# A four-layer graph network on one core: ones multiplied first, x rows a group ahead, feeds put off, ranks before a layer's end, the 20-row block first

## The chip, the cores and the metric

The kernel runs on one core of one Trainium2 chip. The metric is the time of one execution on the device in microseconds; the median over several runs is given. The core's engines, each with its own queue of instructions, are TensorE (PE in the profile; its weight loads are PEld), VectorE (DVE), ScalarE (ACT), GpSimd (POOL) and SyncE (SP, which here only issues DMAs).

## The reference, cut to what matters

```python
# x: 2708 x 512 float32; adj: 2708 x 2708 of zeros and ones, symmetric, some 16 ones in a row
deg = max(sum(adj != 0, axis=-1), 1)
# layer 0
dinv = rsqrt(deg); a_norm = dinv * (adj + I) * dinv
x = layernorm(x + relu((a_norm @ x + x) @ W0 + b0))
# layer 1
dis = (adj.sum(1) + 1e-8) ** -0.5
x = layernorm(x + ((dis * adj * dis.T) @ x) @ W1.T + b1)
# layer 2: attention, twice
y = x
for W in W2_stack:                       # 512 x 1024 each
    Wh, Ws = split(y @ W, 2, axis=-1)
    y = leaky_relu((softmax(Wh @ Ws.T) * adj) @ Wh + y, 0.01)
x = layernorm(x + y)
# layer 3: eight heads that together are one 512 x 512 matrix
x = layernorm(x + adj @ (x @ W3) + b3)
```

## The kernel before

The 2708 nodes are 22 blocks of 128 rows; the last block, number 21, has only 20 rows in use. The columns of a result (nodes again) are worked on in six chunks (`CH`: four of 512, one of 384, one of 276), and for each chunk the source blocks come in six groups (`GROUPS`: four groups of four blocks, two of three). A step is one (layer, chunk k, group g). `step` (line 1043) writes out the work of every engine for that step by hand, and all instructions go through `OrderedEngine` (line 62; its calls are made in line 70, which is why the profile gives L70 for nearly everything). It ties each instruction to the one written before it on the same engine. So the order within each engine is the order of the program text; no scheduler changes it.

Layers 0, 1 and 3 have the same form. `load` (line 741) starts the DMAs of adjacency tiles `at`, two steps ahead of their use, on SP's queue; in layer 0 these are 256 KB tiles of float32, later pages of bytes from `masks`, which layer 0 writes itself. `prepare` (line 782) runs one step ahead: for each block ACT makes `m`, the adjacency tile in the form in which PE multiplies it; in the first chunk `halve` (line 713) also splits the block's rows x into a high part `xh` (on ACT) and a low part `xl` (on DVE). In layer 0 `examine` (line 814) makes bytes of the tiles (`some` on ACT, `bytes` on POOL), tests them (`odd` on DVE), and adds them up into `part`. In layer 1 `prepare` ends with `feeds`, a DVE reduction that notes which blocks feed which quarters of a block. `multiply` (line 849) then makes the products `acc<-m,xh` and `acc<-m,xl` on PE: four accumulators of a chunk, each a PSUM bank. There are two sets of four banks, used by even and odd chunks in turn.

`load_rows` (line 707) issues the DMAs of the x rows, in layers 0 and 1 on POOL's queue, where weights (`load_weights`, line 697), the residual rows `xres` and the rows `xt` of the transposed x are issued too.

When a chunk's last group is multiplied, `degrees` (line 886, layer 0) makes the degrees: products `deg` and `cnt` on PE, `dg` and `cnt_sb` from them on DVE, then xt times dg on POOL and an inverse square root on DVE. `evict` (line 919) adds accumulators and xt into `ht`. In the next chunk's steps `ends` (line 1079) goes through phases: phase 0 calls `project` (line 936: ht times the weights, `mm`; a block of 20 rows gives four partial sums in one bank), and phases 0 and 1 call `combine` (line 976: scale, bias and residual in `r` and `xres`) and `finish` (line 995: layernorm into `o`, and its DMA). Phase 2 of layer 1 turns the rows for the attention.

Beside layer 1's chunks, and beyond its end, `index` (line 1097) makes the lists by which the attention gathers its neighbours. It is a generator that yields in turn for DVE and for PE: DVE makes `up`, PE the product `rank`; DVE `keep`, `place` and another `up`, PE the product `rest`; DVE `place_r`, a test whose results go to `bad` by way of `top`, and then for each block `at_row`, `hit` and `both` (`one_hot`, line 1221), from which PE makes the product `list`. `work` (line 572) lets the first unfinished job go on by a step. `beat` (line 585) is called once a block in the attention's projections and calls `work` in two of three calls.

The attention's projections (`project_steps`, called in line 1684) make `wst`, which ACT copies, and `z`, whose copy `z_sb` is DVE's. The mixed weights (`mix`) that they need are the first products of the whole program, from weights `wt` that a DMA brings.

After the last layer's last chunk `run` (lines 568 to 570) projects its three blocks 19, 20 and 21, and combines, normalises and stores them one after the other.

Of the kernel before, what the change touches and what calls it, by code (L numbers as in the profile page):

```python
# [8 lines left out]
FP = mybir.dt.float32  # L9
FR = mybir.dt.float32r  # L10
BF = mybir.dt.bfloat16
# [3 lines left out]
ALU = mybir.AluOpType  # L15
# [498 lines left out]
class Fast:  # L514
# [17 lines left out]
    def run(self):  # L532
        kernel, nc = self.k, self.nc
        with ExitStack() as ctx:
            pool = lambda name, bufs, **kw: ctx.enter_context(
                self.tc.tile_pool(name=name, bufs=bufs, reuse_waits="tile", **kw)
            )
            self.pages, self.wides = pool("pages", PAGES), pool("wides", WIDES)
            self.small, self.lists = pool("small_f", 4), pool("lists", 1)
            self.banks = [pool(f"banks{h}", 4, space=PSUM) for h in range(2)]  # L540
            given = [kernel.x_in[bass.ts(i, P), :] for i in range(NB)]
            l0 = Layer(0, given, kernel.w0, kernel.b0)
            l1 = Layer(1, kernel.saved[0], kernel.w1, kernel.b1)
            l3 = Layer(3, kernel.saved[2], kernel.w3, kernel.b3)
            self.attention = attention = Attention(self)
            self.jobs, self.due, self.other, self.beats = [], None, 1, 0
            run = Run(l0, l1)
            for t in range(len(run.seq)):
                self.step(run, t)
            attention.project(attention.layers[0], 0)  # L550
            for g in range(3):
                self.ends(run, g)
                if g == 1:
                    attention.project(attention.layers[0], 1)


            run = Run(l3)
            run.seq = [(l3, k, g) for k in range(TWO) for g in range(4)]
            run.seq += [(l3, k, g) for g in (4, 5) for k in range(2)]
            run.seq += [(l3, k, g) for k in range(2, TWO) for g in (4, 5)]  # L560
            run.seq += [(l3, k, g) for k in range(TWO, len(CH)) for g in range(len(GROUPS))]
            attention.run(self.early(run))
            for j in range(*GROUPS[5]):
                l3.rows[j] = attention.made[j]
            for t in range(4 * TWO, len(run.seq)):
                self.step(run, t)

            ly, k = run.before
            for i, n, ps in self.project(ly, k):
                self.finish(ly, k, [(i, n, self.combine(ly, i, n, ps))])  # L570

    def work(self, engine):

# [131 lines left out]
        nc.gpsimd.dma_start(ly.bt, ly.bias.partition_broadcast(P))  # L705

    def load_rows(self, ly, j):
        if ly.rows[j] is None:
            ly.rows[j] = self.page(f"x{ly.number}_{j}")
            queue = self.nc.sync if ly.number == 3 else self.nc.gpsimd  # L710
            queue.dma_start(ly.rows[j], ly.source[j])
# [29 lines left out]
    def load(self, ly, k, g):  # L741
# [26 lines left out]
            ly.done["bytes", k, g] = at  # L768
        ly.done["at", k, g] = tiles
        if k == 0 and ly.number == 0:  # L770
            for j in range(*GROUPS[g]):
                self.load_rows(ly, j)
        if k == 0 and ly.number == 3 and g < 4:
            for j in range(*GROUPS[g]):
# [4 lines left out]
                self.nc.gpsimd.dma_start(xt[c][:, :cw], self.k.x_t[:, c, c0 : c0 + cw])  # L779
            ly.done["xt", k] = xt  # L780

    def prepare(self, ly, k, g):


        nc, (c0, cw) = self.nc, CH[k]
        ats = ly.done.pop(("at", k, g), None)
        if ats is None:
            return
        ms = []
        for j, at in zip(range(*GROUPS[g]), ats):  # L790
            if k == 0:
                self.halve(ly, j)
            m = self.page(f"m{ly.number}_{k}_{j}", FR)
            nc.scalar.copy(m[:, :cw], at[:, :cw])
            ms.append(m)
        ly.done["m", k, g] = ms
        if ly.number == 0:
            self.examine(ly, k, g, ats)
        if ly.number == 1:
            at, (j0, j1) = ly.done.pop(("bytes", k, g)), GROUPS[g]  # L800
            feeds = self.k.feeds.rearrange("p i q j -> p j (i q)")
            i0, full = c0 // QW, cw // QW
            sets = [(j0, j1, P)] if j1 < NB else [(j0, j1 - 1, P), (j1 - 1, j1, QW)]
            for q0, q1, n in ((0, full, QW), (full, -(-cw // QW), cw % QW)):
                for a, b, rows in sets if q0 < q1 else ():
                    v = at[:rows, a - j0 : b - j0, q0 * QW : q0 * QW + (q1 - q0) * n]
                    nc.vector.tensor_reduce(
                        feeds[:rows, a:b, i0 + q0 : i0 + q1],
                        v.rearrange("p j (q i) -> p j q i", i=n),
                        AX.X,  # L810
                        ALU.max,
                    )

    def examine(self, ly, k, g, ats):
        nc, cw = self.nc, CH[k][1]
# [67 lines left out]
                    stop=(j in stops and not first),  # L883
                )

    def degrees(self, ly, k, g):

        nc, cw = self.nc, CH[k][1]
        i0, n = CH[k][0] // P, len(blocks_of(k))
        if g == len(GROUPS) - 2:  # L890
            ly.both = both = self.page(f"both{k}", BF)
            if cw % P:
                nc.vector.memset(both, 0.0)
            nc.vector.tensor_add(both[:, :cw], ly.part[k][:, 0, :cw], ly.part[k][:, 1, :cw])
            return
        both = ly.both
        ps = self.bank(k + 1, f"deg{k}")
        nc.tensor.matmul(ps[:, :cw], self.k.ones_b, both[:, :cw], start=True, stop=True)
        pc = self.bank(k + 1, f"cnt{k}")
        for q in range(n):  # L900
            nc.tensor.matmul(
                pc[:, q : q + 1],
                both[:, bass.ts(q, P)],
                self.k.ones_b[:, 0:1],
                start=True,
                stop=True,
            )
        dg = self.page(f"dg{k}")
        nc.vector.tensor_scalar(dg[:, :cw], ps[:, :cw], 1.0, 1.0, ALU.max, ALU.add)
        cnt = self.small.tile([P, DC], FP, tag="cnt", name=f"cnt_sb{k}")[:, :n]  # L910
        nc.vector.tensor_copy(cnt, pc[:, :n])
        xt = ly.done["xt", k]
        for c in range(DC):
            nc.gpsimd.tensor_mul(xt[c][:, :cw], xt[c][:, :cw], dg[:, :cw])
# [21 lines left out]
    def project(self, ly, k):  # L936

        nc = self.nc
        parts = []
        for i, lo, n in blocks_of(k):  # L940
            if n <= QW:
                ps = self.few(
                    k,
# [32 lines left out]
    def combine(self, ly, i, n, ps):  # L976

        nc, x = self.nc, ly.done.pop(("xres", i))
        if n <= QW:
            t = self.page(f"mm_sb{ly.number}_{i}")  # L980
            self.total(t[:n], ps, n, D)
            ps = t
# [12 lines left out]
    def finish(self, ly, k, parts):  # L995
# [8 lines left out]
        for i, o, n in out:  # L1004
            if ly.number == 3:
                nc.sync.dma_start(self.k.out[i * P : i * P + n, :], o[:n])
            else:
                rows = n if ly.number else P
                nc.gpsimd.dma_start(self.k.saved[ly.number][i][:rows], o[:rows])
        return out  # L1010

    def before_products(self, run, t):

# [2 lines left out]
        if t == 0:  # L1016
            mixing = self.attention.mix(0)
            next(mixing)
            self.load(*seq[0])
            self.load(*seq[1])  # L1020
            self.k.constants(self.page)
            self.prepare(*seq[0])
        if t + 2 < len(seq):
            self.load(*seq[t + 2])
# [7 lines left out]
        if ly.number == 1 and k == 0 and g == 0:  # L1032
            for j in range(*GROUPS[4]):
                self.load_rows(ly, j)
        if t + 1 < len(seq):
            self.prepare(*seq[t + 1])
        if ly.number == 0 and g == len(GROUPS) - 2:
            self.degrees(ly, k, g)
        if t == 0:
            for _ in mixing:  # L1040
                pass
# [1 line left out]
    def step(self, run, t):  # L1043
# [21 lines left out]
        if g == len(GROUPS) - 1:  # L1065
            if ly.number == 3:
                self.biased(ly, k)
            if ly.number == 0:
                self.degrees(ly, k, g)
            while run.before and run.phase < 2:  # L1070
                self.ends(run, run.phase)
                run.phase += 1
            self.evict(ly, k)
            run.before, run.phase = (ly, k), 0
            if ly.number == 1:
                self.jobs.append((k, self.index(k)))
                self.work("DVE")

    def ends(self, run, g):

        nc, (ly, k) = self.nc, run.before
        if g == 0:
            run.parts = self.project(ly, k)
            run.x = []
        if g in (0, 1):
            some = run.parts[:2] if g == 0 else run.parts[2:]
            run.x += [(i, n, self.combine(ly, i, n, ps)) for i, n, ps in some]
# [9 lines left out]
    def index(self, k):  # L1097
# [79 lines left out]
        )  # L1177
        nc.vector.tensor_add(place, place, place_r)

        top = tile_("top", [P, n], FP)  # L1180
        nc.vector.tensor_mul(place_r, rank, rest[:, :, PAD:])
        nc.vector.tensor_reduce(top, place_r, AX.X, ALU.max)
        for q, (i, _, _) in enumerate(blocks_of(k)):
            room = sum(t >= nq * ONLY for ts in lists_of(i) for t in ts) * P
            nc.vector.tensor_scalar(
                kernel.bad[:, kernel.nbad + i : kernel.nbad + i + 1],
                top[:, q : q + 1],
                1.0 - room,
                0.0,
                ALU.add,  # L1190
                ALU.max,
            )
        whole, part = (self.page(f"{t}{k}", I32, one) for t in ("whole", "part"))
        row, which = tile_("row", one, BF), tile_("which", one, BF)
        nc.vector.tensor_scalar_add(whole, place, float(FAR))
# [4 lines left out]
        sums = tile_("sums", [P, n, 2 * LISTS], FP)  # L1200
        for q in range(n):
            rows, both = self.one_hot(i0 + q, row[:, q, :], which[:, q, :])
            yield "PE"
            ps = self.bank(self.other, f"list{i0 + q}", (P, 2 * LISTS))
            for j in range(NB):
# [69 lines left out]
class Attention:  # L1275
# [98 lines left out]
    def project_steps(self, ly, k):  # L1374
# [19 lines left out]
        for i, lo, n in blocks_of(k):  # L1394
# [8 lines left out]
            for c in range(DC if n > QW else 0):  # L1403
# [4 lines left out]
                    start=(c == 0),  # L1408
                    stop=(c == DC - 1),
                )  # L1410
            if n > QW:
                nc.vector.tensor_copy(z[:n], ps[:n])
            for b in range(2):
                nc.sync.dma_start(
# [429 lines left out]
```

## Time and profile before

| | us |
|---|---|
| timed, median of 3 runs | 2369.26 (2368.26 to 2371.22) |
| profiled execution, its own time | 2338.2 |
| its span | 2336.5 |
| PE busy in it | 2274.8 |
| DVE busy | 1474.8 |
| POOL busy | 762.3 |
| ACT busy | 662.2 |

The span reaches from the first to the last event that the profiler recorded; the profiled execution's own time has 1.7 us more. The profiled execution is another one than the timed ones. Busy times of the engines overlap. In a row of the timeline stand the start, the time, the engine, the line, the operation, output and inputs by their names, shapes and types, a count, and in square brackets the time that the engine was idle before it and what released it. PEclk is the clock that TensorE was granted, as a share of the full one.

In the span, layer 0 lies up to about 319 us, layer 1's products up to about 615, the end of layer 1 with the first attention layer's projections up to about 786. The attention's scores and sums follow, and layer 3 is last.

### The profile page before, as it was taken

What the parts mean: (1) busy time and instruction counts of PE and PEld (TensorE: products, weight loads), DVE (VectorE), ACT (ScalarE), POOL (GpSimd) and SP (SyncE); (2) the same over time, 40 slices, a digit from 0 to 9 for tenths busy, and PEclk for the clock granted to TensorE, in tenths of its full rate; (3) what the DMA queues carried; (4) which work ended last, traced back from release to release, by engine and by line L of the source; (5) the groups of instructions that cost most, each with busy time, mean ns of one, the idle gap of its engine ahead of it and who ended that gap; (6) DMA issues with size and microseconds to landing.
All of it is one profiled execution on the core that took longest, in us unless ns stands there. A gap on an engine that the chain in (4) does not pass through costs nothing.

```text
span 2336.5 us, 26171 instructions
## 1 busy us (share of the span) xinstructions
PE 2274.8 (97%) x8518; PEld 1292.5 (55%) x8518; DVE 1474.8 (63%) x2831; ACT 662.2 (28%) x1334; POOL 762.3 (33%) x879
## 2 busy tenths in 40 slices
PE   8999999999999999999999999999999999999997
PEld 6677677778644444443456444444443456566585
DVE  6999986786655529657677511228677788724523
ACT  6544353223100113222223200113232334432211
POOL 6645641111000000636375550000636466551000
PEclk9999999999999999999999999999999999999998
DMA  9765652222434404869699996405869799983311
GB/s 343 258 199 169 182 172 86 74 86 70 171 146 167 154 0 143 278 229 311 204 324 350 302 388 232 152 0 163 279 217 314 233 316 329 305 279 96 123 48 43
DMA packets 312440, 463.50 MB, mean 198 GB/s; under 512 B 60162, under 2 KB 189706, under 8 KB 312292
## 3 DMA queue, kind: packets, MB, share of 16 engines
q1 hardware_dynamic: 252276, 240.81, 31.5%
q0 software_dynamic: 60016, 220.92, 27.1%
q8 instruction: 69, 1.13, 0.2%
q14 instruction: 79, 0.65, 0.1%
HBM read 307.75 MB, written 153.85 MB: 198 GB/s over the span
## 4 chain that ended last, share of the span: by engine, by line
PE 84%; DVE 7%; DMA 4%; issue 2%; ACT 1%; POOL 1%; SPq 0%; DVEq 0%; ACTq 0%; POOLq 0%
PE sp L70 32%; PE acc L70 29%; PE mm L70 9%; PE z L70 6%; PE wst L70 6%; DMA pairs<-s 1%; DMA at<-in_adj_t 1%; DVE st L70 1%; DMA at<-mask 1%; ACT m L70 1%; DVE s L70 1%; PE list L70 1%; PE mix L70 0%; POOL bytes L70 0%; PE tr_x2t L70 0%
## 5 line engine op out<-in xcount | busy, mean ns | idle before, releaser
L70 POOL DMA_INDIRECT g<-pairs,givers x510 | 516.2, 1012 | 897.0 <-DMA pairs<-s 537.4
L70 PE MATMUL sp<-xs,wst_sb 128*128 128x512 f32 (+3 forms) x2112 | 797.7, 544 | 0.0
L70 PEld LDWEIGHTS sp<-xs,wst_sb 128*128 128x128 f32 (+1 forms) x2112 | 380.0, 186 | 406.8 <-issue 321.9
L70 PE MATMUL acc<-m,xh 128*128 128x512 f32 (+4 forms) x1584 | 571.4, 382 | 13.6 <-ACT m L70 7.0
L70 PE MATMUL acc<-m,xl 128*128 128x512 f32 (+4 forms) x1584 | 553.2, 367 | 1.5 <-DVE xl L70 1.5
L70 PEld LDWEIGHTS acc<-m,xh 128*128 128x128 f32 (+1 forms) x1584 | 290.3, 189 | 81.4 <-issue 22.3
L70 PEld LDWEIGHTS acc<-m,xl 128*128 128x128 f32 (+1 forms) x1584 | 290.3, 189 | 48.1 <-issue 5.7
L70 ACT COPY s<-sp 128x512 f32<-128x512 f32 (+2 forms) x252 | 133.6, 531 | 482.1 <-PE sp L70 469.5
L70 PE MATMUL acc<-g 128*32 128x512 f32 (+1 forms) x1020 | 260.8, 605 | 0.9 <-DMA g<-pairs,givers 0.5
L70 DVE TENSOR_TENSOR top<-top,s 128x512 f32<-128x512 f32 (+5 forms) x240 | 149.6, 623 | 170.6 <-ACT s L70 169.1
L70 PE MATMUL mm<-w,ht 128*128 128x512 f32 (+1 forms) x528 | 222.6, 593 | 8.1 <-DVE ht L70 8.1
L70 ACT CAST m<-at 128x512 fp32r<-128x512 uint8 (+5 forms) x396 | 199.2, 567 | 80.0 <-DMA at<-mask 63.7
L70 ACT ACTIVATE s<-s 128x512 f32<-128x512 f32 (+3 forms) x264 | 150.7, 580 | 236.6 <-DVE s L70 236.3
L70 DVE TENSOR_TENSOR sum<-sum,s 128x512 f32<-128x512 f32 (+4 forms) x252 | 157.4, 625 | 23.9 <-ACT s L70 23.9
L70 DVE TENSOR_TENSOR s<-s,a 128x512 f32<-128x512 f32 (+3 forms) x264 | 165.9, 628 | 10.2 <-DMA a<-mask 1.2
L70 DVE TENSOR_TENSOR s<-s,shift 128x512 f32<-128x512 f32 (+3 forms) x264 | 162.8, 620 | 6.7 <-ACT shift L70 6.7
L70 PEld LDWEIGHTS mm<-w,ht 128*128 128x128 f32 (+1 forms) x528 | 95.5, 186 | 124.4 <-issue 110.9
L70 PE MATMUL wst<-xt,mixed 128*128 128x512 f32 (+2 forms) x384 | 152.5, 550 | 1.7 <-ACT mixed L70 1.7
L70 PEld LDWEIGHTS acc<-g 128*32 128x32 f32 (+1 forms) x1020 | 75.4, 134 | 136.9 <-issue 115.8
L70 PE MATMUL z<-w,xt 128*128 128x512 f32 (+1 forms) x352 | 151.0, 596 | 0.0
L70 DVE COPY z_sb<-z 128x512 f32<-128x512 f32 (+1 forms) x44 | 30.3, 690 | 179.5 <-PE z L70 176.3
L70 POOL DMA_DIRECT2D x<-o x44 | 26.0, 596 | 358.0 <-DVE o L70 354.2
(167 smaller groups left out, 1657.4 us busy)
## 6 DMA issues: line engine op xcount, KB each, us to landing
pairs<-s SPq DMA_DIRECT2D x378, 128.0 KB
pairs<-z_sb SPq DMA_DIRECT2D x84, 512.0 KB
at<-in_adj_t SPq DMA_DIRECT2D x84, 256.0 KB
xres<-x POOLq DMA_DIRECT2D x44, 256.0 KB, 4.3
x<-o POOLq DMA_DIRECT2D x43, 256.0 KB, 3.1
x<-x SPq DMA_DIRECT2D x37, 256.0 KB
at<-mask SPq DMA_DIRECT2D x32, 256.0 KB
xt<-t SPq DMA_DIRECT2D x32, 256.0 KB
```

Source lines behind the costliest of these rows:

```text
L70: ins = call(*args, **kw)
```

## The change

- At the program's start DVE fills a page with ones and PE multiplies it with itself seven times, ahead of the mix products.
- In layer 0's first chunk, `load` issues the x rows of group g+1 together with group g's tiles, from g = 2 on; those of group 2 follow right after the constants. The transfers and their number are the same, their places in POOL's queue are earlier.
- At the passage from layer 0 to layer 1, layer 1's first group is no longer prepared ahead of layer 0's last products but between parts of `degree_ends`: products deg and cnt, the first block's xh, xl and m, then dg and cnt_sb, then the other three blocks, then the square roots.
- The reductions `feeds` of layer 1 are kept in `put_off` and written at the end of the step.
- In `ends` of layer 1's last chunk, `beat` is called once after the projection, ahead of `combine`; every later call in the attention's projections so comes one place further on in its cycle.
- In `index` the test into `bad` moves behind the first block's `one_hot`.
- `project` takes a block of 20 rows first, and `finish` returns its blocks in the order of their numbers. In layer 3 `combine` adds such a block's four partial sums straight to the residual instead of copying and adding them up first. At the very end blocks 21 and 19 are normalised together, and block 20 after them.
- In the first attention layer the copies `z_sb` of 128 rows go from DVE to ACT; those of 20 rows stay on DVE.

The diff, cut to its core:

```diff
@@ run
             ly, k = run.before
-            for i, n, ps in self.project(ly, k):
-                self.finish(ly, k, [(i, n, self.combine(ly, i, n, ps))])
+            parts = self.project(ly, k)
+            for some in (parts[:-1], parts[-1:]):
+                self.finish(ly, k, [(i, n, self.combine(ly, i, n, ps)) for i, n, ps in some])
@@ load_rows
-        if ly.rows[j] is None:
+        if ly.rows[j] is None and ly.hi[j] is None:
@@ load
         if k == 0 and ly.number == 0:
-            for j in range(*GROUPS[g]):
+            for j in range(GROUPS[g][0], GROUPS[min(g + (g > 1), len(GROUPS) - 1)][1]):
                 self.load_rows(ly, j)
@@ prepare(self, ly, k, g, between=None)
             nc.scalar.copy(m[:, :cw], at[:, :cw])
             ms.append(m)
+            if between:
+                between()
+                between = None
...
         if ly.number == 1:
-            at, (j0, j1) = ly.done.pop(("bytes", k, g)), GROUPS[g]
...
+            at = ly.done.pop(("bytes", k, g))
+            self.put_off.append(lambda: self.note(k, g, at))   # note: the same reductions
@@ degrees is split; the second half is degree_ends
+        yield True                       # after the products deg and cnt
         dg = self.page(f"dg{k}")
         nc.vector.tensor_scalar(dg[:, :cw], ps[:, :cw], 1.0, 1.0, ALU.max, ALU.add)
         cnt = self.small.tile([P, DC], FP, tag="cnt", name=f"cnt_sb{k}")[:, :n]
         nc.vector.tensor_copy(cnt, pc[:, :n])
+        yield True
         xt = ly.done["xt", k]
@@ project
-        for i, lo, n in blocks_of(k):
+        for i, lo, n in sorted(blocks_of(k), key=lambda b: b[2] > QW):
@@ combine
+        if n <= QW and ly.number == 3:
+            for c in range(DC):
+                nc.vector.tensor_add(x[:n], x[:n], ps[c * QW : c * QW + n, :])
+            return x
@@ finish
-        return out
+        return sorted(out, key=lambda b: b[0])
+
+    def begin(self):
+        nc, t = self.nc, self.page("begin", BF)
+        nc.vector.memset(t, 1.0)
+        ps = self.bank(0, "begin")
+        for _ in range(7):
+            nc.tensor.matmul(ps, t[:, :P], t[:, :BANK], start=True, stop=True)
@@ before_products
             next(mixing)
+            self.begin()
             self.load(*seq[0])
             self.load(*seq[1])
             self.k.constants(self.page)
+            for j in range(*GROUPS[2]):
+                self.load_rows(ly, j)
             self.prepare(*seq[0])
...
-        if t + 1 < len(seq):
+        if t + 1 < len(seq) and seq[t + 1][0].number == ly.number:
             self.prepare(*seq[t + 1])
@@ step, after a chunk's last group
             if ly.number == 0:
-                self.degrees(ly, k, g)
+                ends = self.degree_ends(ly, k)
+                next(ends)
+                if k == len(CH) - 1:
+                    self.prepare(*run.seq[t + 1], between=lambda: next(ends))
+                for _ in ends:
+                    pass
...
+        while self.put_off:
+            self.put_off.pop(0)()
+        if g == len(GROUPS) - 1:
             if ly.number == 1:
@@ ends
             run.parts = self.project(ly, k)
             run.x = []
+            if ly.number == 1 and k == len(CH) - 1:
+                self.beat()
@@ index: top and bad become examine(), and
             rows, both = self.one_hot(i0 + q, row[:, q, :], which[:, q, :])
+            if q == 0:
+                examine()
             yield "PE"
@@ project_steps
-            if n > QW:
+            if n > QW and a == 0:
+                nc.scalar.copy(z[:n], ps[:n])
+            elif n > QW:
                 nc.vector.tensor_copy(z[:n], ps[:n])
```

More of the change, by code (lines that the diff above doesn't have):

```diff
@@ L546, in run @@
             self.jobs, self.due, self.other, self.beats = [], None, 1, 0
+            self.put_off = []
             run = Run(l0, l1)
@@ L780, in load, with prepare @@
             ly.done["xt", k] = xt
-    def prepare(self, ly, k, g):
+    def prepare(self, ly, k, g, between=None):
         nc, (c0, cw) = self.nc, CH[k]
@@ L799, in prepare, with note @@
         if ly.number == 1:
-            at, (j0, j1) = ly.done.pop(("bytes", k, g)), GROUPS[g]
[L801 to L812, printed above, removed]
+            at = ly.done.pop(("bytes", k, g))
+            self.put_off.append(lambda: self.note(k, g, at))
+    def note(self, k, g, at):
+        (c0, cw), (j0, j1) = CH[k], GROUPS[g]
+        feeds = self.k.feeds.rearrange("p i q j -> p j (i q)")
+        i0, full = c0 // QW, cw // QW
+        sets = [(j0, j1, P)] if j1 < NB else [(j0, j1 - 1, P), (j1 - 1, j1, QW)]
+        for q0, q1, n in ((0, full, QW), (full, -(-cw // QW), cw % QW)):
+            for a, b, rows in sets if q0 < q1 else ():
+                v = at[:rows, a - j0 : b - j0, q0 * QW : q0 * QW + (q1 - q0) * n]
+                self.nc.vector.tensor_reduce(
+                    feeds[:rows, a:b, i0 + q0 : i0 + q1],
+                    v.rearrange("p j (q i) -> p j q i", i=n),
+                    AX.X,
+                    ALU.max,
+                )
     def examine(self, ly, k, g, ats):
@@ L884, in multiply, with degrees, degree_ends @@
                 )
-    def degrees(self, ly, k, g):
+    def degrees(self, ly, k):
         nc, cw = self.nc, CH[k][1]
-        i0, n = CH[k][0] // P, len(blocks_of(k))
[L890 to L896, printed above, removed]
+        ly.both = both = self.page(f"both{k}", BF)
+        if cw % P:
+            nc.vector.memset(both, 0.0)
+        nc.vector.tensor_add(both[:, :cw], ly.part[k][:, 0, :cw], ly.part[k][:, 1, :cw])
+    def degree_ends(self, ly, k):
+        nc, cw, both = self.nc, CH[k][1], ly.both
+        i0, n = CH[k][0] // P, len(blocks_of(k))
         ps = self.bank(k + 1, f"deg{k}")
@@ L1034, in before_products @@
                 self.load_rows(ly, j)
-        if t + 1 < len(seq):
+        if t + 1 < len(seq) and seq[t + 1][0].number == ly.number:
             self.prepare(*seq[t + 1])
         if ly.number == 0 and g == len(GROUPS) - 2:
-            self.degrees(ly, k, g)
+            self.degrees(ly, k)
         if t == 0:
@@ L1068, in step @@
             if ly.number == 0:
-                self.degrees(ly, k, g)
+                ends = self.degree_ends(ly, k)
[4 more added lines that the diff above has]
+                    pass
             while run.before and run.phase < 2:
@@ L1178, in index, with examine @@
         nc.vector.tensor_add(place, place, place_r)
[L1180 to L1192, printed above, removed]
+        def examine():
+            top = tile_("top", [P, n], FP)
+            nc.vector.tensor_mul(place_r, rank, rest[:, :, PAD:])
+            nc.vector.tensor_reduce(top, place_r, AX.X, ALU.max)
+            for q, (i, _, _) in enumerate(blocks_of(k)):
+                room = sum(t >= nq * ONLY for ts in lists_of(i) for t in ts) * P
+                nc.vector.tensor_scalar(
+                    kernel.bad[:, kernel.nbad + i : kernel.nbad + i + 1],
+                    top[:, q : q + 1],
+                    1.0 - room,
+                    0.0,
+                    ALU.add,
+                    ALU.max,
+                )
         whole, part = (self.page(f"{t}{k}", I32, one) for t in ("whole", "part"))
```

## The prediction

> **What bounds the kernel now.** First the page.
>
> ```profile
> span 2336.5 us, 26171 instructions
> PE 2274.8 (97%) x8518; PEld 1292.5 (55%) x8518; DVE 1474.8 (63%) x2831; ACT 662.2 (28%) x1334; POOL 762.3 (33%) x879
> PEclk9999999999999999999999999999999999999998
> ```
>
> TensorE is busy for 97% of the span, so nothing hidden behind it pays. Against the change stand only PE's idle time, its time at a lower clock, and the tail after its last product. The waits view, PE alone, names the idle time (total, times, longest):
>
> ```profile
> PE mm L70 <- DVE ht L70: 8.1, 4, 2.6
> PE acc L70 <- ACT m L70: 7.0, 5, 2.9
> PE mix L70 <- DMA wt<-in_w_t: 4.3, 1, 4.3
> PE list L70 <- DVE both L70: 4.2, 3, 2.7
> PE rest L70 <- DVE up L70: 4.1, 1, 4.1
> PE acc L70 <- DVE dg L70: 3.6, 1, 3.6
> PE rank L70 <- DVE up L70: 0.6, 1, 0.6
> ```
>
> PE's timeline places them: list at 413.1 (1.24), 747.0 (0.32) and 790.0 (2.68), rest at 663.65, dg at 309.4, the longest "ACT m" at 56.3, rank at 773.7, ht at 73.6 (2.26) and again in layer 3. The windows view (us; busy PE, PEld, DVE, ACT and POOL; PEclk; DMA share; GB/s) tells what such a hole costs besides itself:
>
> ```profile
> 24.00:48.00 24.00, 24.00 (x107) 19.88 (x106) 23.03 (x41) 18.17 (x35) 18.97 (x28) 1.00 1.01 370
> 300.00:320.00 20.00, 16.43 (x100) 14.06 (x99) 16.92 (x43) 14.19 (x30) 17.81 (x30) 0.91 0.95 314
> 660.00:680.00 20.00, 15.90 (x39) 6.64 (x38) 13.88 (x45) 2.34 (x5) 1.81 (x3) 0.91 0.16 63
> ```
>
> A clock of 0.91 over 20 us is 1.7 us lost (0.09 x 20): one stretch of some 3.4 us at half speed after a hole. In the matmul rows I find six, after the holes at 56, 309, 413, 663 and two of layer 3's. So a hole removed can be worth its idle time and 1.7 us. The first row shows the other limit: in the first chunk DVE is busy 23.03 of 24 us.
>
> **What the Trainium skill says.** "TensorE: Matmul & The Clock Gate", section "What's actually happening": PE starts at half rate, returns to it after an idle window of about 3.4 us, and is raised after a busy one; the window is free-running. The trace agrees: the mix products start .85 us apart and stand .43 apart from 9.7 on. It differs in that holes of 1.24 us were followed by half speed too, so which hole is punished is luck. "PSUM — Partial Sum Buffer", section "Engine vs sequencer instructions": the queues of ScalarE, VectorE and GpSimdE are strict FIFO; here keep waits behind an unrelated layernorm though rank was ready long before. "SBUF — State Buffer", section "Who interferes with whom": VectorE and GpSimd share a port pair under an exclusive lock; DVE's odd takes 0.69 us alone and 1.40 to 1.53 where a POOL cast lies beside it.
>
> **The change, part by part.** Gains are positive.
>
> *Ones first, x ahead.* Seven bf16 products (7 x 0.43 us at half clock = 3.0) stand in the 4.35 us in which PE waits for wt. They use up the slow window, so mix, 4.35 to 20.41, ends about 1.6 earlier. The x rows of group g+1 are issued with group g; now the later ones come late:
>
> ```profile
> 49.38 0.63 ACT L70 ACTIVATE xh<-x 128x512 fp32r<-128x512 f32 x1 [2.58 <-DMA x<-in_x]
> ```
>
> Everything on this chunk is also in DVE's order, idle only some 2 us between 42 and 59. So group 5 starts at about 57.6 instead of 59.23, and the hole of 2.95 shrinks to 1.3, probably without its half clock. But after the chunk PE must wait for ht, which hangs on dg (68.86), POOL's four xt (69.64 to 74.6) and DVE's small operations. DVE's work up to there is unchanged and moves up at most 1.4 us, so the ht hole grows from 2.26 to about 4.4, and may get a half clock of its own. Unseen before: four x rows (1 MB, 2.6 us at the 400 GB/s that 9 to 21 us show) competing with the first adjacency tiles. Bounds -2.5 (they delay everything) to +3 (all of it is kept, clock too); I take 0.
>
> *Layer 0 to 1.* Now PE waits 3.57 for dg, which stands behind layer 1's first xl and feeds:
>
> ```profile
> 307.46 2.88 DVE L70 SCALAR_TENSOR_TENSOR xl<-x,dis,xh 128x512 fp32r<-128x512 f32 x4
> 310.27 2.28 DVE L70 TENSOR_REDUCE feeds<-at 128x64 bf16<-128x2048 uint8 x1
> 312.46 0.43 DVE L70 TENSOR_SCALAR dg<-deg 128x276 f32<-128x276 f32 x1
> 344.46 2.72 DVE L70 SCALAR_TENSOR_TENSOR xl<-x,dis,xh 128x512 fp32r<-128x512 f32 x4
> ```
>
> With dg and cnt_sb after one xl instead of four and feeds, banks come free by about 308.9 and PE's first group ends near 315.5, not 319. It then needs ht, and ht needs POOL's product, whose place behind three mask casts and the DMA issues of w and bias is unchanged:
>
> ```profile
> 316.55 3.01 POOL L70 TENSOR_TENSOR xt<-xt,dg 128x276 f32<-128x276 f32 x4
> ```
>
> ht_0 comes at about 317.8 (a hole of 2.3), and the 20-row block, now first, needs the last ht (320.04). The projection ends near 327.3 instead of 329.0. Then the next wait: before xl_12 (the row at 344.46; first of them ready at 345.15) DVE has the same 32.7 us of work plus some 5 us of waits for ht and mm, since put-off feeds of the steps in between still lie ahead of it. xl_12 is ready near 346.1, PE gets there at 342.2: a hole of 3.9 with a half clock, where now it is 1.20 without. Against 345.25 before that is 0.85 + 1.7 = 2.6 lost: **-2.6**, bounds -4 (both holes slow) to +2 (DVE's waits close up).
>
> *List at 413.* The six small operations of examine (0.84 us) leave the path to both, so 1.24 becomes 0.4 and the half clock at 416 probably goes: 0.84 + 1.4, **+2.2** (0.8 if the clock stays, 2.9 at most).
>
> *Ranks ahead of layer 1's end.* rank ends at 645.3, yet:
>
> ```profile
> 653.60 0.67 DVE L70 COPY mm_sb<-mm 20x512 f32<-20x512 f32 x1
> 663.27 0.53 DVE L70 SCALAR_TENSOR_TENSOR keep<-rank,up 128x352 bf16<-128x352 f32 x1
> 666.53 1.17 DVE L70 TENSOR_TENSOR up<-up 128x88 bf16<-128x88 bf16 x5
> ```
>
> keep to up is 4.5 us. Put right after the projection it is done near 650, in time for rest, which PE now reaches at 663.65 and after the change a step sooner, near 660. The 4.10 us and the half clock after it go: **+5.8**. What is pushed back is combine and layernorm, 4.5 us later; behind them on ACT, in order, stand rs_t (till about 665) and the next wst and z copies, but PE has four banks to go on with, until about 667. The first both is ready near 668.3 where PE wants it at 670.5: 2 us of slack. If that slack is missed, one hole of up to 4.5 returns; bounds +1 to +6.
>
> *z copies.* 21 copies of 128x512 move from DVE (0.69 us) to ACT (0.59 for its copy of this size). ACT has 13.2 of 150 us busy from 640 to 790, so 21 x 0.59 = 12.4 us fit. DVE is 14.5 us freer, and with examine later the holes at 747 (0.32), 773.7 (0.56) and 790 (2.68) go: **+3.5** (1 to 3.6).
>
> *The end.* The last product ends at 2318.9; the rest is DVE, for block 21 last of all:
>
> ```profile
> 2323.34 2.12 DVE L70 TENSOR_TENSOR mm_sb<-mm_sb,mm 20x512 f32<-20x512 f32 x3
> 2328.51 0.53 DVE L70 TENSOR_SCALAR o<-xres,mv,y 20x512 f32<-20x512 f32 x1
> ```
>
> Now 21 goes first in PE and DVE, its copy and three adds and add (3.5 us) become four adds (2.8) beside PE's other blocks, and 19 and 21 share a layernorm. Block 20 alone is left: from its mm at 2318.9, with DVE free at 2321.4, add .69, statistics .87, square root and four small ones 1.6, o .55: 2325.0, against 2329.04. The last DMA is 256 KB instead of 40 KB, of whose 7.4 us to the span's end I add 0.2: **+3.8** (2.8 to 4.2).
>
> *At no cost.* Feeds at a step's end: the same 2.28 us of DVE, hidden behind PE in layer 1; without cover each would cost at most its 2.28. The mid-layer order of blocks, 20 rows first, only swaps products.
>
> Sum: 0 - 2.6 + 2.2 + 5.8 + 3.5 + 3.8 = **+12.7**. The profiled execution took 2338.2 (span 2336.5 and 1.7 around it), so 2325.5. The median of the three timed runs, 2369.26, lies 31.1 above it, and I keep that distance: 2356.6, rounded to **2356.5**.
>
> **Rivals.** (1) *The start is kept too.* The half clocks at 60.9 and at the transition vanish and DVE closes up: 3 at the start, 2.6 + 2 at the transition, so some 7 more, 2349.5. For it: the ACT waits for x are real. Against: DVE's 23 of 24 us.
> (2) *The ranks' gain turns into new waits.* Lists come 2 us late, ACT's in-order copies hold a bank: of 5.8 + 3.5 some 2 remain, and the start's DMA costs 2.5. 12.7 - 7.3 - 2.5 = 2.9, that is 2366, no difference. For it: the slack is only 2 us. Against: DVE and ACT are mostly idle there.
> (3) *Slower.* Put-off feeds hold each layer-1 mask page to the end of its step, and the pool has 82 pages. A new `at` load then waits for a page, m comes late on ACT, and PE stands still in each step. There are 36 steps; the 12.7 are used up at 0.35 us a step, and at 0.5, 18 us, the kernel is at 2374.6 or so, clock losses not counted. Against: a step takes 9 us (323 us over 36) and loads go out two steps ahead, and before the change PE waits for m only five times in all.
> (4) *It doesn't do what it says*: PE's order, set by other waits, leaves the 663 hole. Then 12.7 - 5.8 = 6.9: 2362.4.
>
> **Chances.** Forecast with its own range of 2350 to 2362: 0.58. Rival 1: 0.14; rival 4: 0.08; rival 2: 0.13; rival 3: 0.07. About 0.2%, 4.7 us, is what a measurement here can tell from no change, so faster means under 2364.5. Faster takes the forecast, rivals 1 and 4 and a fifth of rival 2: 0.83; same 0.11; slower rival 3 less a little: 0.06. The range goes to rival 1 with its own spread below and rival 2 above: 2345 to 2367.
>
> **What would show it.** In the waits of PE: rest gone, dg gone, list and rank under 1 us, ht up from 8.1 to some 10 to 14, xl up from 1.5 to about 4. In the windows: 660 to 680 at 1.00. DVE's keep near 646, the last o near 2325 less the gain ahead of it. ACT about 12 us busier, DVE 14 less. The prediction is wrong if rest still waits, if PE waits for m in layer 1's steps, or if PE's idle time does not fall by some 10 us.

## The result: a little slower, where a gain of 13 us was forecast

| | before | changed |
|---|---|---|
| timed, median of 12 runs each, us | 2368.2 | 2374.77 |
| ratio, 95% interval | | 1.0019 (1.0003 to 1.0035) |
| span of the profiled execution, us | 2336.5 | 2376.4 |

By the ratio the changed kernel is 4.5 us (0.7 to 8.3) slower. Its page:

```profile
span 2376.4 us, 26202 instructions
PE 2293.5 (97%) x8525; PEld 1298.8 (55%) x8525; DVE 1458.0 (61%) x2804; ACT 671.7 (28%) x1354; POOL 761.7 (32%) x879
```

The spans differ by 40 us; the timed runs differ by 4.5 us by the ratio and by 6.6 by the medians. So the two spans can't simply be subtracted. A table by stage tells why. It is made from the starts of PE's own products in the traces, named as in the profile; the third column is the unchanged kernel profiled once more (experiment 1), the last the changed kernel.

| stage, from the start of one product to the start of another | before, us | before again | changed |
|---|---|---|---|
| start to deg of layer 0's second chunk | 121.4 | 122.4 | 123.4 |
| deg of layer 0's last chunk to layer 1's first mm | 61.7 | 59.8 | 62.7 |
| layer 1's first rest to its second mm chunk (the list at 413) | 21.7 | 20.8 | 20.8 |
| second rest to fourth rank | 166.7 | 166.7 | 182.3 |
| fourth rank to the attention's first tr_top | 226.5 | 226.5 | 216.3 |
| that tr_top to layer 3's first mm (attention) | 1271.5 | 1292.5 | 1306.2 |
| last chunk's mm to the end of the span | 24.5 | 24.5 | 22.1 |

The change touches nothing in the attention, and there the unchanged kernel too took 21 us more when it was profiled again. In two of the three sets of experiments the timed runs of before have medians of 2369 and 2370 us, in the third 2341, and the first profiled execution is of the level of the third. Each set ran on another chip (experiments 1 to 4, then 5, 6, 7 and 9, then 8, 10 and 11), so the level may go with the chip; no run separates the chip from the time of the set, and the chip of the first profiled execution is not on record. Ratios hold within a set; across sets only stages outside the attention are compared below. Against the mean of the two columns of before, those stages give +1.5, +2.0, -0.4, +15.6, -10.2 and -2.4: 6.1 us, inside the interval of the timed runs.

One row decides: 15.6 us lost between layer 1's second rest and its fourth rank, a stretch in which the prediction saw nothing at all. The changed kernel's waits of PE (total, times, longest):

```profile
PE mm L70 <- DVE ht L70: 10.9, 5, 3.0
PE acc L70 <- DVE place_r L70: 10.0, 2, 5.2
PE acc L70 <- DVE xl L70: 7.9, 7, 2.1
...
PE list L70 <- DVE both L70: 1.8, 2, 1.4
...
PE begin L70 <- DVE begin L70: 1.5, 1, 1.5
PE mix L70 <- DMA wt<-in_w_t: 0.9, 1, 0.9
```

Of the waits that the prediction wanted gone, rest, dg and rank are no longer there, list fell from 4.2 to 1.8 (the holes at 747 and 790 went, the first at 413 shrank), and mix from 4.3 to 0.9. In the second row is a wait that was not there before: accumulators waiting for place_r, 10.0 us in two holes of 5.22 and 4.75. PE's timeline has the first of them, in brackets the idle time and what ended it:

```profile
485.86 0.39 PE L70 MATMUL acc<-m,xl 128*128 128x512 f32 x1
491.47 0.79 PE L70 MATMUL acc<-m,xh 128*128 128x512 f32 x1 [5.22 <-DVE place_r L70]
```

The windows around both holes, and the one of the forecast's largest gain (us; busy PE, PEld, DVE, ACT, POOL; PEclk; DMA share; GB/s). First the changed kernel, then the first two windows in the kernel before:

```profile
480.00:500.00 20.00, 14.71 (x47) 9.59 (x46) 12.51 (x28) 4.33 (x9) 0.00 (x0) 0.83 0.08 23
590.00:610.00 20.00, 15.25 (x58) 9.95 (x58) 10.11 (x25) 3.06 (x9) 0.00 (x0) 0.83 0.35 111
660.00:680.00 20.00, 20.00 (x56) 8.44 (x55) 15.54 (x40) 2.01 (x5) 0.49 (x1) 1.00 0.28 109
```

```profile
480.00:500.00 20.00, 20.00 (x61) 11.26 (x60) 16.76 (x31) 2.00 (x4) 0.00 (x0) 1.00 0.05 14
590.00:610.00 20.00, 20.00 (x147) 16.75 (x146) 17.10 (x35) 5.12 (x16) 4.49 (x8) 1.00 0.66 210
```

PEclk 0.83 over 20 us is 3.4 us lost to the clock in each of the changed kernel's first two rows, a part of it within the hole itself. In its third row, 0.91 has become 1.00 and PE is busy throughout: that gain came as foreseen.

What place_r has to do with an accumulator stands on DVE, in the same stretch:

```profile
483.20 2.27 DVE L70 TENSOR_REDUCE feeds<-at 128x64 bf16<-128x2048 uint8 x1
485.40 0.23 DVE L70 SCALAR_TENSOR_TENSOR place_r<-rest,up 128x88 f32<-128x88 f32 x1
...
487.03 3.22 DVE L70 TENSOR_TENSOR at_row<-upto,row 128x1024 bf16<-128x1024 bf16 x3
...
490.83 0.43 DVE L70 TENSOR_TENSOR both<-hit,block 128x264 bf16<-128x264 bf16 x1
491.17 0.24 DVE L70 TENSOR_TENSOR place_r<-rest,up 128x88 f32<-128x88 f32 x1
```

place_r is written twice from the PE product that the profile calls `rest`: once for the place and once for the test into bad. That product lies in a PSUM bank, of the set of four that the next chunk's accumulators need. (In the code the bank is the variable `rank`; the code's `rest` is the other operand, `up` in the profile.) The change moves the test behind the first one_hot, and the second read with it, from 0.6 us after the first to 5.8 us after. The bank comes free at 491.4, and PE starts at 491.47. In the kernel before the same two reads were:

```profile
481.38 0.24 DVE L70 SCALAR_TENSOR_TENSOR place_r<-rest,up 128x88 f32<-128x88 f32 x1
...
481.94 0.25 DVE L70 TENSOR_TENSOR place_r<-rest,up 128x88 f32<-128x88 f32 x1
```

### The profile page after: what moved, and what is told of

The parts are those of the page before. It is cut to its first block, busy times and chain, and to the rows that moved or that the text cites. A ratio compares the mean times of both kernels' runs of the same rounds, so it can differ in the third digit from the quotient of the medians.

```text
span 2376.4 us, 26202 instructions
## 1 busy us (share of the span) xinstructions
PE 2293.5 (97%) x8525; PEld 1298.8 (55%) x8525; DVE 1458.0 (61%) x2804; ACT 671.7 (28%) x1354; POOL 761.7 (32%) x879
## 4 chain that ended last, share of the span: by engine, by line
PE 84%; DVE 7%; issue 3%; DMA 2%; ACT 2%; POOL 1%; another core or an unknown queue 0%; SPq 0%; DVEq 0%; POOLq 0%; ACTq 0%
PE sp L70 31%; PE acc L70 29%; PE mm L70 8%; PE wst L70 6%; PE z L70 6%; DVE odd L70 1%; DMA at<-in_adj_t 1%; DVE st L70 1%; DVE r L70 1%; DVE feeds L70 1%; DMA g<-pairs,givers 1%; DVE at_row L70 1%; PE list L70 1%; ACT m L70 0%; DVE xl L70 0%
## 5 line engine op out<-in xcount | busy, mean ns | idle before, releaser
L70 PE MATMUL acc<-m,xh 128*128 128x512 f32 (+4 forms) x1584 | 571.7, 382 | 21.4 <-DVE place_r L70 10.0
L70 PE MATMUL mm<-w,ht 128*128 128x512 f32 (+1 forms) x528 | 231.0, 607 | 10.9 <-DVE ht L70 10.9
L70 DVE TENSOR_TENSOR sum<-sum,s 128x512 f32<-128x512 f32 (+4 forms) x252 | 156.9, 622 | 40.8 <-ACT s L70 22.1
L70 DVE SCALAR_TENSOR_TENSOR odd<-at 128x512 bf16<-128x512 f32 (+2 forms) x132 | 118.2, 895 | 2.1
```

What stands on the lines that cost most here:

```text
L70: ins = call(*args, **kw)
```

## The experiments

**1. The kernel before, again.** No edit.

> The kernel before, once more, for its trace beside the others. Theory A (the attention's own stalls): in the trace of the changed kernel, 35 us more than in the trace of before came up between 1220 and 2125 us, in the attention, whose code is the same; if that is in every execution of either kernel, this one takes about 2368 and shows some 30 us more than the first trace of before between its first sp product (786.3) and the end of the attention, and the same as that one ahead of 786. Rival (the change does it): this execution takes about 2338 like the first profiled one.

Measured: span 2355.6, between the two; 1.8 us less than the first trace up to the attention, and 21 more in it. So the attention's extra time is not the change's doing. In the other traces of the first two sets it was 22 to 35 us more than in the first trace of before, with PE idle at about the same few places; in those of the third it was between 1 us less and 3 more. DVE and then PE at one of its places, in the unchanged kernel:

```profile
1229.49 0.56 DVE L70 TENSOR_REDUCE mx<-tr_top 128x3 f32<-128x384 f32 x1 [7.85 <-remote]
```

```profile
1230.78 0.87 PE L70 MATMUL tr_mx<-ident,wide 128*128 128x128 f32 x3 [5.61 <-issue]
```

tr_top, on which DVE's row depends, had ended at 1224.6. DVE did nothing for 4.9 us more, and the profile shows no releaser ("remote", "issue"). What stops it stays open.

**2. The test back in its old place.**

```diff
--- changed kernel
+++ experiment
-        def examine():
-            top = ...; place_r = rank * rest; the tests into bad
+        top = ...; place_r = rank * rest; the tests into bad
...
-            if q == 0:
-                examine()
```

> The changed kernel with the test into bad back in its old place, ahead of the first one_hot. Theory B (a bank held): the late test reads the PSUM bank of rest some 5 us later, and PE needs that bank for the fourth accumulator of the next chunk; the holes at 486 (5.22) and 594 (4.75) and the half clock after each, 15.7 us together, go, and 1 to 2 us at the lists come back: 14 us less than the changed kernel, ratio to before 0.995 to 0.998. Rival O (DVE is late because the feeds lie ahead of place_r): the holes stay within 1 us, ratio 1.001 to 1.003.

Measured: ratio 0.9939 (0.9919 to 0.996). Between the second rest and the fourth rank 167.1 us, as before the change, and no wait of PE at all from 470 to 610. The feeds still lie ahead of place_r here, so rival O falls. The timed gain over the changed kernel, some 19 us of the ratios' difference, is larger than the 14 expected, but the intervals allow 14 as well.

**3. Only the bank freed.** One operation is moved, 0.25 us long: the one that reads the bank.

```diff
--- changed kernel
+++ experiment
+        nc.vector.tensor_mul(place_r, rank, rest[:, :, PAD:])
+
         def examine():
             top = tile_("top", [P, n], FP)
-            nc.vector.tensor_mul(place_r, rank, rest[:, :, PAD:])
             nc.vector.tensor_reduce(top, place_r, AX.X, ALU.max)
```

> The changed kernel, where only the product of rank and rest, the one operation of the late test that reads the bank, is made early; the reduction and the tests into bad stay late. Theory B: the holes at 486 and 594 go as in the experiment with the whole test back, and the lists keep their gain: ratio to before 0.994 to 0.997. Rival O: no different from the changed kernel, 1.001 to 1.003.

Measured: ratio 0.9948 (0.9927 to 0.9969), the stretch 167.0 us. The bank is the operand `rank` in this code. The row of DVE that frees it, and the two windows:

```profile
485.96 0.25 DVE L70 TENSOR_TENSOR place_r<-rest,up 128x88 f32<-128x88 f32 x1
```

```profile
480.00:500.00 20.00, 19.92 (x64) 11.43 (x63) 17.64 (x33) 4.33 (x9) 0.00 (x0) 1.00 0.08 23
590.00:610.00 20.00, 20.00 (x132) 15.21 (x131) 16.74 (x39) 3.99 (x13) 3.46 (x7) 1.00 0.63 195
```

Five operations of the test stay late, and nothing is lost: the cause is not their order but the bank's last reader. Theory B is shown.

**4. The late test alone, on the kernel before.** The reverse of the edit of experiment 2.

> The kernel before, with the test into bad behind the first one_hot and nothing else changed. Theory B: the bank of rest comes free at about 487.2 and 587.9 where PE wants it at 484 and 584.5: two holes of about 3.3 us, each with some 2.5 us at half clock, less 1 to 2 us won at the lists: 9 us slower, ratio 1.003 to 1.005. Rival O: without the feeds put off there is no hole; 1 to 3 us faster, ratio 0.999.

Measured: ratio 1.0043 (1.003 to 1.0057), 177.7 us for the stretch instead of 166.7. PE's waits from 480 to 610:

```profile
PE acc L70 <- DVE place_r L70: 7.0, 2, 3.5
```

Two holes of 3.5, and 4.0 us more, most of it the half clock after them. In the changed kernel the first hole is 1.7 us longer because the put-off feeds stand ahead of the first place_r as well (2.27 us in the timeline above): that row comes 5.0 us after the product rest there, and 3.2 here. The list stage took 20.8 us here, as in "before again": the late test won nothing there. From the fourth rank to the first tr_top it won 1.2 us (225.3 for 226.5).

**5. Ranks ahead and z copies on ACT, alone.**

```diff
--- before
+++ experiment
             run.x = []
+            if ly.number == 1 and k == len(CH) - 1:
+                self.beat()
...
-            if n > QW:
+            if n > QW and a == 0:
+                nc.scalar.copy(z[:n], ps[:n])
+            elif n > QW:
                 nc.vector.tensor_copy(z[:n], ps[:n])
```

> The kernel before with the beat ahead of layer 1's last combine and the z copies on ACT, nothing else. Theory B's other half (the prediction's steps for these two, 5.8 and 3.5, stand): between the fourth rank and the attention's first tr_top the trace shows 216 us, as the changed kernel does, where the kernel before has 226.5: 10 us less, ratio 0.9945 to 0.997. Rival: the gain there needs the late test and the feeds put off as well; then 4 to 6 us, ratio 0.997 to 0.9985, with holes at the lists of 747 to 793 left.

Measured: ratio 0.9959 (0.9941 to 0.9976); 216.3 us for the stretch, all of the gain, without the other parts. The rival, that the late test is needed as well, falls. PE waits for nothing from 600 to 800. keep and the end of up on DVE, and the window:

```profile
645.25 0.53 DVE L70 SCALAR_TENSOR_TENSOR keep<-rank,up 128x352 bf16<-128x352 f32 x1 [6.45 <-PE rank L70]
...
648.52 1.17 DVE L70 TENSOR_TENSOR up<-up 128x88 bf16<-128x88 bf16 x5
```

```profile
660.00:680.00 20.00, 20.00 (x70) 9.22 (x69) 19.00 (x44) 4.23 (x9) 1.82 (x3) 1.00 0.37 142
```

up is done at 649.7; the prediction had put it "near 650".

**6. The 20-row block first, alone** (project, combine of layer 3, the last finish, as in the diff above).

> The kernel before with the 20-row block first in project, its shorter combine in layer 3 and the last finish in two parts. Theory: from the last chunk's first mm to the end of the span 24.5 us become about 21, that is 3 to 4.5 us less, and the other chunks' ends stay as they are: ratio 0.998 to 0.9992. Rival: the larger last DMA (256 KB for 40 KB) and the later last product take it back: ratio 0.9995 to 1.0005.

Measured: ratio 0.996 (0.9947 to 0.9973), 9.5 us and more than expected. The end gives 3.1 us (21.4 instead of 24.5). 4.9 us more come from a place that prediction and expectation held to be untouched, the wait of rest:

```profile
658.27 0.51 DVE L70 SCALAR_TENSOR_TENSOR keep<-rank,up 128x352 bf16<-128x352 f32 x1
```

```profile
PE rest L70 <- DVE up L70: 0.9, 1, 0.9
```

In layer 1's last chunk the small block's copy and adds now run while PE still makes the others, so the whole layernorm, and keep behind it, end earlier; the wait fell from 4.1 to 0.9 and no half clock followed. This overlaps with the ranks' gain: with both edits (experiment 10) the stretch takes the same 216.3 us as with the ranks alone.

**7. The passage from layer 0 to layer 1, alone** (degree_ends, between, and the condition in before_products).

> The kernel before with only the passage from layer 0 to layer 1 re-ordered (deg and cnt ahead of layer 1's first xl, dg and cnt_sb after one of them). The prediction's step: PE's wait for dg goes, waits for ht and xl_12 come; layer 1's second projection starts 1 to 4 us later than in the kernel before (369 to 370), slower by that: ratio 1.0005 to 1.0015. Rival: the loss that the changed kernel shows there (about 2.5) comes from the feeds put off; then the passage alone gains 1 to 3 us, ratio 0.999.

Measured: ratio 0.9992 (0.9978 to 1.0006). The stage took 61.2 us, against 59.0 to 61.7 for the eight traces without this edit and without the feeds put off: neither a loss nor a gain that can be told, so this run decides between neither expectation. The wait for dg (3.6 in the trace of before) is gone, a wait for ht (2.1) has come, and the one for xl is 1.5 instead of 1.2.

**8. The feeds put off, alone** (note and put_off).

> The kernel before with only the feeds of layer 1 put off to the end of their step. Theory P: the changed kernel's passage into layer 1 is some 2 us slower than that of the kernel with the passage alone re-ordered, and the put-off feeds, which stand ahead of xl_12 and of place_r, are why; here dg comes 2.3 us earlier, the wait for xl_12 grows from 1.2 to 2 to 4 us, and no hole of over 1 us comes up in the chunks after: ratio 0.9993 to 1.001. Rival (slower mechanism of the prediction: the mask pages are held too long): waits of PE for m in layer 1, 10 us or more, ratio above 1.004.

Measured: ratio 1.0014 (1.0007 to 1.0022), 62.9 us for the stage. DVE just ahead of xl_12, and PE's wait for it:

```profile
344.56 2.27 DVE L70 TENSOR_REDUCE feeds<-at 128x64 bf16<-128x2048 uint8 x1
346.76 2.72 DVE L70 SCALAR_TENSOR_TENSOR xl<-x,dis,xh 128x512 fp32r<-128x512 f32 x4
```

```profile
PE acc L70 <- DVE xl L70: 3.7, 1, 3.7
```

In the kernel before xl followed the layernorm directly (344.46) and PE waited 1.2. So, as far as one trace each can tell, it is the feeds and not the passage that make this stage slower. PE waited for m once in layer 1, for 0.5 us, and the stretch from second rest to fourth rank took 167.1 us: the prediction's slower rival, pages held too long, does not occur.

**9. Products of ones and x rows a group ahead, alone** (begin, and the loads).

> The kernel before with the products of ones at first and layer 0's x rows a group ahead. The prediction's step: mix ends 1 to 1.5 us earlier, the x rows come in time, and DVE, full over the chunk, gives it all back before ht: the first mm at 75.5 to 77, as before (75.8 to 76.8), ratio 0.9995 to 1.0005. Rival (start is kept): first mm at 73 or earlier, ratio 0.998 to 0.999.

Measured: ratio 1.0012 (0.9999 to 1.0025); the first mm at 77.1, the latest of all traces, if only just (74.7 to 76.9 in the nine without this edit, 76.1 to 77.0 in the three others with it). The largest of PE's waits up to 80 us is now for xl, which DVE makes; in the window below DVE, the third of the busy times, is at 35.72 of 36 us (34.04 in "before again"). So rival "start is kept" falls:

```profile
PE acc L70 <- DVE xl L70: 3.4, 3, 2.1
```

```profile
24.00:60.00 36.00, 34.02 (x149) 26.70 (x147) 35.72 (x61) 32.48 (x65) 27.48 (x39) 1.00 0.93 338
```

**10. What gained, together** (edits of 5 and 6 on the kernel before).

> The parts that gained, alone: ranks ahead, z copies on ACT and the 20-row block first, on the kernel before; the test into bad in its old place, no products of ones, x rows, passage and feeds as before. If the parts add up as in the sum: 10.3 us between the fourth rank and the attention, 3.5 at the end, 14 us less than the kernel before, ratio 0.993 to 0.9955. Rival (they overlap with what the other parts give): no better than the changed kernel with its test back, 0.995 to 0.9965.

Measured: ratio 0.9952 (0.9936 to 0.9967). Both expected ranges hold this, so the time alone does not decide. The trace shows the gains overlap: 216.3 us for the stretch, as with the ranks alone, and 2.4 us at the end.

**11. The same with the bank freed and the rest of the test late** (edit of 3 as well).

> As the run with ranks and tail, but with the product that reads the bank made early and the rest of the test late. By the measured list holes the late test gains 0 to 1 us in all, so no difference can be told from that run: ratio 0.993 to 0.9955, and no hole at the fourth accumulators of the next chunks. Rival (the prediction's step for the lists, 2.2 us): 0.992 to 0.9945 and a list wait below 1 us in all.

Measured: ratio 0.9935 (0.992 to 0.995), the lowest of all, but not to be told from experiments 2, 3 and 10. Its waits of PE from 300 to 800 are down to two:

```profile
PE acc L70 <- DVE dg L70: 2.5, 1, 2.5
PE list L70 <- DVE both L70: 1.7, 2, 1.1
```

The lists' wait is 1.8 in experiment 10. Against the kernel before, this version is some 15 us faster by its ratio (12 to 19), and that of experiment 10 some 11 (8 to 15).

## Why the prediction was wrong, point by point

- **The failed step is "List at 413".** It took the six operations of the test for 0.84 us of DVE that leave a path, and priced the move as a gain of 2.2 and "0.8 if the clock stays" at worst. It didn't ask what the moved operations read. One reads a PSUM bank, so moving it lengthened the bank's use by 5.2 us (485.96 in experiment 3, 491.17 in the changed kernel); where the next chunk's accumulators come soon after, PE stood still for 5.22 and 4.75 us, and most of the other 5.6 us of the 15.6 went to the half clock: 6.83 us of it with each hole, of which 4.6 and 6.0 us lie after the hole's end and cost half, 5.3 in all. Experiments 3 and 4 show it from both sides. The gain at 413 was nothing that can be told: the list stage takes 20.8 us with the late test and 20.8 without (before again). What the first list wins, the second one loses: 1.37 us of waiting at 422, where before again waited 0.61. Only the half clock behind the first list may be a gain: it came in three of the nine traces with the early test, where the stage then takes 21.7, and in none of the four with the late one.
- **Put-off feeds were "at no cost".** They cost 3.3 us (1.6 to 5.2, experiment 8); what the trace shows of it is at the very place, xl_12, that the passage's step described. That step named the feeds too and put -2.6 for both together; the stage took 62.7 us in the changed kernel, 64.8 and 64.1 in experiments 2 and 3, against a mean of 60.7 over the eight traces without either edit: 2 to 4 us. That step was right in size and in the next wait that it named; on these traces the part that causes it is the feeds. They also lengthened the two holes for the bank (experiment 4).
- **Ranks and z copies, +5.8 and +3.5:** measured 10.2, and the same alone (experiment 5). The late test, which the prediction counted in for the holes at 747 to 790, is not needed for it. The new waits of rival 2 did not come.
- **The end, +3.8:** 2.4 in the changed kernel, 2.4 to 4.3 over the six traces with this edit. What was missed is that the 20-row block first helps layer 1's end too; beside the ranks it adds nothing there.
- **The start, 0:** mix ends at 19.6, 19.8, 20.7 and 22.2 in the four traces with the edit, against 20.3 to 21.3; ACT's waits for x are gone; and nothing of it reaches the first mm, which DVE, busy throughout, sets. The sum was right, one wait in it was not: the hole for ht at the first mm was put at about 4.4 and stayed at 1.9 to 2.2, and the waits went to xl instead. The 1.5 us in the table's first row go with a half clock after that hole (at 76.2), which came at this place in two traces without the edit too.
- **The distance of 31.1 us** between the profiled execution and the timed ones was taken for a constant of the measurement. It was a different level of the attention's time; the ratio doesn't depend on it, but a comparison of whole spans does. What sets the level stays open.
- With 15.6 and the 2.2 that didn't come taken off, the sum of +12.7 becomes -5.1; measured is -4.5 (-0.7 to -8.3). The other terms were off by up to 1.5 us each and in part cancel, so that closeness is partly luck.

The rivals missed it in kind: (3) was slower by a buffer held too long, but it was a page of SBUF and not a bank of PSUM, and not in this place. That its example gave 2374.6, beside the measured 2374.77, is chance. Of the prediction's own signs of being wrong, neither a wait for rest nor waits for m in layer 1's steps came. The third did: PE's holes of over 0.25 us up to 800 us add up to 29.4 us, against 27.0 before, so they did not fall by 10. None of the three names the wait for place_r.

## What to carry to other kernels

When an instruction is moved later, list what it reads and who writes there next. The last read of a PSUM bank is also its release, and with four banks to a set, as here, its lateness can cost more than the path that it leaves: here 15.6 us for 0.84. If only part of a deferred block reads the bank, do that read in its old place and defer the rest. Compare traces stage by stage, from one product to the same product, before explaining a difference of spans.

## What the runs showed of the hardware that was not expected

- With the holes of 5.22 and 4.75 us on PE came 6.83 us at half clock each, which began 2.3 and 0.9 us before the hole's end; after each 3.5 us hole of experiment 4 came 3.41 us. The hole of 1.24 us at the first list was followed by 3.41 us at half clock in three of nine traces, the first of before among them, and by none in the others, before again among them.
- The same attention took from 1270 to 1307 us. In the traces of the first two sets, and in that of the changed kernel, it was 1292 to 1307 us, with holes of PE of some 3 to 6 us, in which DVE and ACT mostly wait too and POOL goes on issuing gathers; in the first trace of before and in the three of the third set it was 1270 to 1274. The difference goes with the set and its chip, and not with the edit.
